# Attention tiles of a Mamba-attention-MoE kernel: the 64-row products of group 0 issued ahead of the 32-row products of groups 1 and 2

## The chip, the cores and the metric

The kernel runs on one core of a Trainium2 chip. A core has five engines that run side by side and meet at semaphores: TensorE (PE; its loads of weights are shown as PEld), VectorE (DVE), ScalarE (ACT), GpSimd (POOL) and SyncE (SP), which issues most DMAs. Each executes its own instructions in the order in which the program gives them. TensorE writes to PSUM, which has 8 banks of 128 partitions x 512 float32 values here; VectorE and ScalarE read it. The metric is the device time of one execution in microseconds (us), as the median of several runs. All data is float32.

## The reference

A state-space convolution layer (Mamba) is followed by an additive attention and a mixture of experts, over 8 batches of 4096 tokens with 128 channels. The change lies in the attention:

```
f = x @ W1[:h];  g = x @ W1[h:]
t = tanh(f[:, :, None, :] + g[:, None, :, :] + b1)      # 16 hidden units
scores = einsum('bija,a->bij', t, w2) + b2
e = exp(scores) * strictly_lower_triangle
w = e / (sum(e) + 1e-10)
out = w @ x
```

Every pair of a query token i and an earlier token j needs a sum over 16 values of tanh.

## The kernel before

The kernel does not compute the tanh. It writes the sum over the hidden units as a sum of three fractions N/D, one for each group of hidden units: group 0 has six units (64 sign patterns), groups 1 and 2 have five each (32 patterns). For each pair of tokens D is a product of exponentials, expanded to a sum over the sign patterns; so D and N are matrix products over 64 or 32 rows: `V` (one column per earlier token j) against `U` (one column per query i). The vectors are made in the first part (`mamba`, up to about 1,900 us of the span), kept in DRAM and brought back by `bring`.

`attend` (from about 1,907 to 6,062 us) works through 1,088 tiles of 128 earlier tokens x 512 queries, 136 per batch. 64 of them, on the diagonal, have only 256 columns; others near the diagonal are put together from two pieces. The order of the work is written out by hand; nothing reorders it. The loop at the end of `attend` runs over i, and an iteration works on several tiles:

- `rounds(cur, nxt)`, line 624 on TensorE: the D products of tile i+2 and the N products of tile i, six in all (each is a weight load and a product in two passes). In `V` and `U` the 64 rows of group 0 stand twice, at partitions 0 to 63 for D and 64 to 127 for N. The 32-row vectors stand at 0 to 31 (group 1, D), 32 to 63 (group 1, N), 64 to 95 (group 2, D) and 96 to 127 (group 2, N). Products in different rows of the array can run side by side: four with 32 rows, or two with 64.
- `inverses`, on ScalarE: line 643 takes the logarithm of the two D12 banks, line 644 that of the D0 bank, and line 646 (649 and 652 where the widths differ) takes exp(-x) of the three logarithms and of the scores of tile i-1 together.
- `causal`, line 666 on VectorE: the mask, on diagonal tiles.
- `ratios` and `scores`: line 657 (VectorE) multiplies the inverses of groups 1 and 2 by N12, line 658 (VectorE) that of group 0 by N0, line 659 (GpSimd) adds the fractions of groups 1 and 2, and line 671 (VectorE) adds that of group 0 to the sum.
- `weigh`, line 680 on TensorE: the weights of tile i-3 times the tokens, added up in the bank `av`.

Ahead of `rounds`, `advance("v", 3)` lets up to three steps of other work run, mostly on VectorE (finishing a block of queries, layer norm, the routing of the mixture of experts: lines 702 to 863); `advance("p", 1)` behind `weigh` issues at most one step on TensorE (lines 750, 720, 782, 845, 852).

PSUM is full: D12 and N12 (the products of groups 1 and 2) have two banks each, D0 and N0 (group 0) one each, `av` one and the other work one. Each has a single buffer. So a product into a bank waits until the reader of the iteration before is done: D12 for line 643, N12 for line 657, D0 for line 644, N0 for line 658. The readers in turn wait for the products: lines 643 and 657 for the group-2 product of their kind, the last into its banks.

After the attention come the experts and the output (from 6,062 us).

Of the kernel before, what the change touches and what calls it, by code (L numbers as in the profile page):

```python
# [44 lines left out]
def fast_path(  # L45
# [538 lines left out]
    def attend(aw, small, ap):  # L584
# [23 lines left out]
        def rounds(cur, nxt):  # L608


            parts = [(i, which) for i, which in ((nxt, 0), (cur, 1)) if i is not None]
            for i, which in parts:
                s = "DN"[which]
                (den, num)[which][i] = (
                    ap.tile([P, 2, CH], F32, tag=f"{s}12", name=f"{s}12_{i}"),
                    ap.tile([P, CH], F32, tag=f"{s}0", name=f"{s}0_{i}"),
                )
            for g, ab, rows, k in ((1, 1, 0, 32), (2, 1, 64, 32), (0, 0, 0, 64)):
                for i, which in parts:
                    b, ic, pieces = tiles[i]  # L620
                    r = slice(rows + k * which, rows + k * (which + 1))
                    t12, t0 = (den, num)[which][i]
                    for jb, q, n, at in pieces:
                        nc.tensor.matmul(  # L624
                            t12[:, g - 1, at : at + n] if g else t0[:, at : at + n],
                            lhsT=V[b, jb // NQ][r, ab, ts(jb % NQ, P)],
                            rhs=U[b, ic][r, ab, q : q + n],
                            start=True,
                            stop=True,
                        )  # L630
# [428 lines left out]
        for i in range(-2, n + 3):  # L1059
            cur = i if 0 <= i < n else None  # L1060
            nxt = i + 2 if i + 2 < n else None
            last = i - 1 if 0 <= i - 1 < n else None
            if 0 <= i < n:
                b, at = divmod(i, per)
                for more, g in begin.get(at, []):
                    if b + more < B:
                        bring(b + more, g)
            if i == -2:
                room(-2)
            if i < n:  # L1070
                room(i + 1)
            advance("v", 3)
            rounds(cur, nxt)
            if nxt is not None or last is not None:
                inverses(i, nxt, last)
            if i >= 2 and i - 2 < n:
                causal(i - 2)
            if cur is not None:
                ratios(cur)
                scores(cur)  # L1080
            if i >= 3:
                weigh(i - 3)
            advance("p", 1)
# [696 lines left out]
```

## Time and profile before

| what | value |
|---|---|
| median of 3 runs | 6327.22 us (6325.18 to 6329.36) |
| the profiled execution: its time | 6327.88 us |
| its span, first to last instruction | 6326.2 us, mean TensorE clock 0.946 |
| TensorE (PE) busy | 5825.4 us, 92% |
| VectorE (DVE) busy | 4935.0 us, 78% |
| ScalarE (ACT) busy | 4987.7 us, 79% |
| GpSimd (POOL) busy | 2023.4 us, 32% |

Windows of the profile, busy us of each engine in the stretch:

| window, us | PE | DVE | ACT | POOL | granted PE clock |
|---|---|---|---|---|---|
| 500 to 1000 (mamba) | 425.98 | 479.95 | 355.18 | 179.72 | 0.88 |
| 3000 to 3500 (attention) | 490.27 | 381.55 | 440.03 | 162.35 | 1.00 |
| 5000 to 5500 (attention) | 488.52 | 382.85 | 439.07 | 160.40 | 1.00 |

The lines of the profile read as follows. A group's line names line of the kernel, engine, operation, the tile written and those read with shapes, and how many; then busy us in all, mean ns of one, the idle us of the engine just ahead of them, and what ended that idle time. A line in order of time has start, duration, engine, line and operation; equal ones that follow each other are merged ("x2"), and in brackets stands the engine's idle time just before and its releaser. A float32 product shows as two instructions, one per pass. Busy time is counted from start to a modelled end for products, so TensorE can look fuller than it is.

### The profile page before, as it was taken

The page shows a single profiled execution, that of the slowest core. Times are in us where ns is not written, and L with a number is a line of the kernel's source. Part 1 is how long each engine was busy: PE and PEld are TensorE (multiplying, and loading weights), DVE is VectorE, ACT ScalarE, POOL GpSimd, SP SyncE. Part 2 cuts the span into 40 slices and gives each one's busy share as a digit, 9 for nine tenths or more (in the row PEclk, how much of TensorE's full clock was granted, in tenths as well). Part 3 has the DMA queues.
Part 4 walks back from the last instruction along what each step waited for, and adds up shares of the span by engine and source line. Part 5 has one row for each costly group of instructions (what it writes and reads, how often), then busy time and mean ns, then how long its engine had stood idle before and what let it go on. Part 6 is the DMA issues. An engine that isn't in the chain of part 4 may idle for free. (4 is left out here: it accounts for less than half of the span.)

```text
span 6326.2 us, 69220 instructions
## 1 busy us (share of the span) xinstructions
PE 5825.4 (92%) x22458; PEld 2224.5 (35%) x22458; DVE 4935.0 (78%) x7955; ACT 4987.7 (79%) x5657; POOL 2023.4 (32%) x1652
## 2 busy tenths in 40 slices
PE   7888888888869999999999999999999999999987
PEld 2333333333323333333333333333333333343335
DVE  7899999999956777777777777777777777777751
ACT  5667767767757998898899889889889988988941
POOL 2333333333312333333233233233333323323311
PEclk8888888888878999999999999999999999999989
DMA  2233333333341010101101101101100110110058
GB/s 81 74 110 117 125 122 126 122 127 127 115 145 60 24 44 26 32 12 49 29 24 32 37 21 44 34 24 31 38 21 24 40 38 24 32 34 24 15 190 303
DMA packets 182407, 426.64 MB, mean 67 GB/s; under 512 B 32579, under 2 KB 33235, under 8 KB 171283
## 3 DMA queue, kind: packets, MB, share of 16 engines
q1 hardware_dynamic: 172514, 403.48, 19.5%
q0 software_dynamic: 9376, 18.37, 0.8%
q8 instruction: 180, 2.95, 0.2%
q14 instruction: 193, 1.57, 0.1%
q10 hardware_dynamic: 144, 0.26, 0.0%
HBM read 295.12 MB, written 126.88 MB: 67 GB/s over the span
## 5 line engine op out<-in xcount | busy, mean ns | idle before, releaser
L624 PE MATMUL D<-U,V 32*128 32x512 f32 (+7 forms) x6912 | 2719.6, 606 | 15.6 <-DMA U<-uv_dram 13.3
L624 PE MATMUL N<-U,V 32*128 32x512 f32 (+7 forms) x6912 | 2354.7, 605 | 51.8 <-DVE mix L657 49.5
L659 POOL TENSOR_TENSOR mix<-mix 128x512 f32<-128x512 f32 (+1 forms) x1088 | 1350.0, 1241 | 2825.9 <-DVE mix L657 2702.7
L646 ACT ACTIVATE mix<-mix 128x2048 f32<-128x2048 f32 x973 | 1853.3, 1905 | 31.1
L671 DVE TENSOR_TENSOR mix<-mix,mix 128x512 f32<-128x512 f32 (+1 forms) x1088 | 736.5, 677 | 916.6 <-POOL mix L659 916.3
L643 ACT ACTIVATE mix<-D 128x1024 f32<-128x1024 f32 (+1 forms) x1088 | 1077.4, 990 | 440.2 <-PE N L624 391.7
L624 PEld LDWEIGHTS D<-U,V 32*128 32x128 f32 (+1 forms) x6912 | 879.4, 185 | 1420.0 <-issue 516.8
L657 DVE TENSOR_TENSOR mix<-mix,N 128x1024 f32<-128x1024 f32 (+1 forms) x1088 | 1284.2, 1180 | 29.5 <-PE N L624 22.8
L680 PE MATMUL av<-mix,tok 128*128 128x512 f32 (+3 forms) x2304 | 1208.9, 611 | 31.1 <-DVE sums L689 29.9
L624 PEld LDWEIGHTS N<-U,V 32*128 32x128 f32 (+1 forms) x6912 | 708.1, 184 | 274.0 <-DVE mix L657 237.5
L658 DVE TENSOR_TENSOR mix<-mix,N 128x512 f32<-128x512 f32 (+1 forms) x1088 | 722.0, 664 | 1.9 <-PE N L624 1.3
L644 ACT ACTIVATE mix<-D 128x512 f32<-128x512 f32 (+1 forms) x1088 | 632.3, 581 | 13.9 <-PE N L624 10.2
L680 PEld LDWEIGHTS av<-mix,tok 128*128 128x128 f32 x2304 | 350.8, 189 | 802.1 <-issue 691.1
L392 POOL TENSOR_TENSOR hc<-hs,rep 128x1024 f32<-128x1024 f32 x192 | 453.2, 2362 | 551.0 <-issue 377.4
L386 DVE TENSOR_TENSOR_SCAN hs<-da,hs,db 128x512 f32<-128x512 f32 x336 | 412.6, 1269 | 18.4 <-ACT da L373 10.0
L399 PE MATMUL py<-hc,ident 128*128 128x512 f32 x768 | 369.2, 633 | 0.9 <-ACT dt L337 0.9
L373 ACT ACTIVATE da<-dt,aneg 128x512 f32<-128x512 f32 x384 | 258.8, 687 | 122.8 <-DVE dt L352 79.9
L279 PE MATMUL px<-xt,wtap 128*128 128x512 f32 x512 | 346.7, 814 | 3.3 <-DMA xt<-in_x_dram 3.3
L326 PE MATMUL pdt<-bc,wdt 8*128 8x512 f32 x256 | 180.0, 824 | 138.7 <-DVE prod L320 85.8
L399 PEld LDWEIGHTS py<-hc,ident 128*128 128x128 f32 x768 | 166.7, 217 | 231.3 <-issue 219.8
L313 POOL DMA_DIRECT2D bc_dram<-bc x128 | 69.1, 544 | 512.8 <-ACT bc L311 512.8
L377 DVE TENSOR_TENSOR db<-dx,rep 128x1024 f32<-128x1024 f32 x192 | 228.0, 1215 | 0.1
(241 smaller groups left out, 5430.3 us busy)
## 6 DMA issues: line engine op xcount, KB each, us to landing
rep<-bc_dram SPq DMA_DIRECT2D x64, 1536.0 KB, 7.0
uv_dram<-uv SPq DMA_DIRECT2D x64, 768.0 KB, 3.5
xr<-in_x_dram SPq DMA_DIRECT2D x64, 256.0 KB, 3.3
k_dram<-tt SPq DMA_DIRECT2D x64, 256.0 KB, 7.2
k_dram<-tok SPq DMA_DIRECT2D x64, 256.0 KB, 7.3
U<-uv_dram SPq DMA_DIRECT2D x128, 128.0 KB, 2.9
V<-uv_dram SPq DMA_DIRECT2D x128, 128.0 KB, 2.9
U<-uv_dram SPq DMA_DIRECT2D x256, 64.0 KB, 2.0
```

The source lines that it names most:

```text
L386: nc.vector.tensor_tensor_scan(hs[:, h, :], ch[c].pop(("da", n, h)), db[:, h, :], first, ALU.mult, ALU.add)
L392: nc.gpsimd.tensor_tensor(hc, ch[c]["hs", n], ch[c]["rep"][:, 1, n, :].unsqueeze(1).to_broadcast([P, 2, CH]), ALU.mult)
L399: nc.tensor.matmul(py, lhsT=ident, rhs=ch[c]["hc", n][:, h, :], start=n == 0, stop=n == NR - 1)
L624: nc.tensor.matmul(t12[:, g - 1, at : at + n] if g else t0[:, at : at + n], lhsT=V[b, jb // NQ][r, ab, ts(jb % NQ, P)], rhs=U[b, ic][r, ab ...
L643: nc.scalar.activation(x[:, 1:3, lo:], d12[:, :, lo:], AF.Ln)
L644: nc.scalar.activation(x[:, 0, lo:], d0[:, lo:], AF.Ln)
L646: nc.scalar.activation(x[:, :, lo:], x[:, :, lo:], AF.Exp, scale=-1.0)
L657: nc.vector.tensor_tensor(r[:, 1:3, lo:], r[:, 1:3, lo:], n12[:, :, lo:], ALU.mult)
L658: nc.vector.tensor_tensor(r[:, 0, lo:], r[:, 0, lo:], n0[:, lo:], ALU.mult)
L659: nc.gpsimd.tensor_tensor(mix[k + 1][:, 3, lo:], r[:, 1, lo:], r[:, 2, lo:], ALU.add)
L671: nc.vector.tensor_tensor(s, s, mix[k - 2][:, 0, lo:], ALU.add)
L680: nc.tensor.matmul(av[0][:, q : q + n], lhsT=tok[b, jb // NQ][:, jb % NQ, :], rhs=mix[k + 1][:, 3, at : at + n], start=first, stop=last,)
```

## The change

One line in `rounds` changes: the order of the three groups. Group 0, the pair of 64-row products into D0 and N0, comes first; the 32-row products of groups 1 and 2 into D12 and N12 follow. The number and the sizes of the products, the banks and the readers stay; the order of the instructions on VectorE, ScalarE, GpSimd and SyncE is the same as before. On TensorE each iteration goes D0, N0, D1, N1, D2, N2, av where it went D1, N1, D2, N2, D0, N0, av.

```diff
-            for g, ab, rows, k in ((1, 1, 0, 32), (2, 1, 64, 32), (0, 0, 0, 64)):
+            for g, ab, rows, k in ((0, 0, 0, 64), (1, 1, 0, 32), (2, 1, 64, 32)):
                 for i, which in parts:
                     b, ic, pieces = tiles[i]
                     r = slice(rows + k * which, rows + k * (which + 1))
```

Some waits stand elsewhere for it. The first D0 product waits for line 644, the first N0 product for line 658. The 32-row products keep no wait for ScalarE or VectorE, since lines 643 and 657 come ahead of 644 and 658 on their engines; what is left to them is a wait for TensorE's own products of the tile before. Lines 644 and 658 wait for no product any more: lines 643 and 657 ahead of them wait for products that are issued behind D0 and N0.

## The prediction

> **What bounds the kernel now.** I read the page first, then the attention stretch (1,919 to 6,062 us, two thirds of the span) by groups of one shape, by waits, and in order of time. The chain that ended last is no help: it goes back only to 6,302 us. TensorE looks like the bound (98% busy in every attention window), but its busy time is modelled, and a product that has been issued early and stands alone counts as much as four that run side by side. So I ask each engine what it waits for. Groups by line and shape, with idle time and what ended it last in each row:
>
> ```profile
> L646 ACT ACTIVATE mix<-mix 128x2048 f32<-128x2048 f32 x966 | 1845.9, 1911 | 30.8
> L657 DVE TENSOR_TENSOR mix<-mix,N 128x1024 f32<-128x1024 f32 x1024 | 1240.8, 1212 | 29.5 <-PE N L624 22.8 <-ACT mix L649 5.8
> L643 ACT ACTIVATE mix<-D 128x1024 f32<-128x1024 f32 x1024 | 1039.9, 1016 | 427.8 <-PE N L624 379.3 <-PE D L624 25.0 <-DMA tt<-k_dram 12.8
> L671 DVE TENSOR_TENSOR mix<-mix,mix 128x512 f32<-128x512 f32 x1024 | 709.2, 693 | 878.6 <-POOL mix L659 878.4
> L658 DVE TENSOR_TENSOR mix<-mix,N 128x512 f32<-128x512 f32 x1024 | 695.6, 679 | 1.3 <-PE N L624 1.3
> ```
>
> ACT waits for TensorE (428 us ahead of line 643). VectorE almost never does: 29.5 us ahead of line 657 in 1,024 tiles, 1.3 us ahead of line 658. Its only regular idle time is the 0.86 us per tile in which line 671 waits for GpSimd's sum, and that lies inside its own chain 657, 659, 671. So VectorE's sequence sets the pace. One tile without other VectorE work, in order of time:
>
> ```profile
> 2370.95 1.21 DVE L657 TENSOR_TENSOR mix<-mix,N 128x1024 f32<-128x1024 f32 x1
> ...
> 2372.09 0.68 DVE L658 TENSOR_TENSOR mix<-mix,N 128x512 f32<-128x512 f32 x1
> ...
> 2372.13 0.69 PE L624 MATMUL D<-U,V 32*128 32x512 f32 x1
> ...
> 2372.22 0.69 PE L624 MATMUL N<-U,V 32*128 32x512 f32 x1
> ...
> 2373.29 0.69 PE L624 MATMUL D<-U,V 64*128 64x512 f32 x1
> ...
> 2373.62 0.69 DVE L671 TENSOR_TENSOR mix<-mix,mix 128x512 f32<-128x512 f32 x1 [0.85 <-POOL mix L659]
> 2374.23 1.21 DVE L657 TENSOR_TENSOR mix<-mix,N 128x1024 f32<-128x1024 f32 x1
> ...
> 2374.35 1.13 PE L680 MATMUL av<-mix,tok 128*128 128x512 f32 x2
> ```
>
> The reader is to see: the next tile's group-1 N product starts at 2372.22, right behind the end of line 657 (2370.95 + 1.21 = 2372.16) and well before line 658 ends (2372.77). The 64-row products follow 1.07 later, when line 658 is long done. So the N12 banks refill while VectorE works on, and line 657 finds its operand ready: from one line 657 to the next 3.28 us, all VectorE. From the starts of line 657 I count 1,087 intervals, 4,143.0 us, mean 3.81. Of the 1,024 behind a full tile, 420 are under 3.35 (mean 3.28), 128 from 3.35 to 3.80 (mean 3.60), 147 from 3.80 to 4.23 (mean 3.93) and 329 longer (mean 4.63: the routing work that VectorE has in these tiles). Of the 63 behind a tile of 256 columns, 47 are under 3.43, mean 3.07.
>
> How long TensorE needs from that N product to line 657 shows only where VectorE really waits:
>
> ```profile
> 2545.28 0.69 PE L624 MATMUL N<-U,V 32*128 32x512 f32 x1
> ...
> 2546.34 0.69 PE L624 MATMUL D<-U,V 64*128 64x512 f32 x1
> ...
> 2546.53 1.02 ACT L643 ACTIVATE mix<-D 128x1024 f32<-128x1024 f32 x1 [1.39 <-PE N L624]
> 2546.58 1.22 DVE L657 TENSOR_TENSOR mix<-mix,N 128x1024 f32<-128x1024 f32 x1 [0.98 <-PE N L624]
> ```
>
> From the 32-row start to line 657 it is 1.30 us, to line 643 1.25, and to the 64-row products 1.06 (two passes of 0.53).
>
> **The change, part by part.** Nothing is added or removed: six products per tile, and the order on VectorE, ScalarE, GpSimd and SyncE is the same; no DMA moves. Only TensorE's order changes, and with it what each wait holds up.
>
> *D0 first.* It waits for line 644 of the iteration before, which reads the only D0 buffer. The 32-row D products need no ACT wait any more, since line 643 ran before 644. Count from T, the start of the 32-row products: line 643 starts at T+1.25, 643 and 644 take 1.49 together (2374.22 to 2375.71 in the same tile, the second starting before the first ends), so D0 starts at T+2.8. TensorE has finished the four 32-row products at T+1.06 and av (1.06, row 2374.35 and the next D at 2375.40) at T+2.12. It then stands still for some 0.7 us. Queued behind D0 are all other products, av among them.
>
> *N0 second.* It waits for line 658 of the tile before, the last reader of the only N0 buffer, and the group-1 and group-2 products stand behind it on TensorE, which takes its products in order (D of 2372.13 went, N waited for line 657 and what follows waited with it). This closes a ring that was not there: line 657 to the end of 658, 2372.77 - 2370.95 = 1.82, I take 1.81 as the median; release of a bank to the N product 0.06 (2372.16 to 2372.22); N0 1.06; 32-row products to the next line 657 1.30. Sum 1.81 + 0.06 + 1.06 + 1.30 = 4.23 us. N0 starts at T+3.17, later than D0, so the N ring decides, not ACT (whose own three rows take 3.34 back to back).
>
> *What the ring covers.* Line 671 and the routing work run inside it, up to 4.23 - 3.28 = 0.95 us of routing per tile. An interval becomes the larger of 4.23 and what it is now. 420 x (4.23 - 3.277) = 400; 128 x (4.23 - 3.603) = 80; 147 x (4.23 - 3.930) = 44; the 329 longer ones nothing, as VectorE's own work covers the ring there; if that cover is partly wait, they would come down instead, by 132 us at most (329 x 0.40). Behind narrow tiles 657 and 658 take 1.01, so the ring is 3.43: 47 x 0.36 = 17. Together 542 us.
>
> *Other TensorE work* (pav, transposes, pl) fits in the idle 0.7 to 1.05 us before N0. Only the 28 groups of sixteen line-852 products (1.89 us) do not: N0 at T+4.0, interval 5.1 against 4.87 now, 28 x 0.25 = 7 us.
>
> *Gains.* Lines 644 and 658 find D0 and N0 early: idle of 13 and 1 us goes, but both now stand inside waiting rings, so I credit nothing.
>
> *The one unseen price* is a switch from 64-row to 32-row products. The seen switches (32 to 64 at 1.06 after a start, 64 to av 1.06, av to 32 1.06) are two bare passes, so zero to 0.01. Below nothing is excluded, since two passes cannot take less than 1.05. I take 0, and as upper end a ring of 4.40, which also covers a slightly lower clock: 683 us. Shortest latencies (ring 4.18): 505 us.
>
> [...]
>
> The profiled execution took 6327.9 us (span 6326.2), 0.7 above the median of 6327.2. 542 + 7 = 549 on the median gives 6876 us.
>
> **The clock.** The granted clock follows how busy TensorE is in a short stretch (columns: window, TensorE busy, clock, DMA share, GB/s):
>
> ```profile
> 1017.00:1020.40 3.40, 2.61 (x6) 1.00 0.62 230
> 1020.40:1023.80 3.40, 1.51 (x3) 0.83 0.21 51
> 1023.80:1027.20 3.40, 3.40 (x5) 0.50 0.96 275
> ```
>
> 77% busy keeps full clock, 44% is followed by half clock. In the new ring TensorE stands still some 0.7 of 4.23 us, 83% busy, so I expect 0.99 to 1.00 as now.
>
> **Rivals.**
> 1. *Clock falls.* The mamba stretch, 79 to 85% busy, has a mean of 0.87. Against: there the idle time comes in pieces of several us. At 0.87 the 2.2 us of products in the ring become 2.5, ring 4.56: +823 us, 7157 with the 7. Decides if windows under about half busy appear. 7%.
> 2. *D0 and N0 do not overlap.* If N0 starts only after D0 ends, T+3.9, the ring is 4.96: +1212 and the 7, 7546. Against: at 2372.13 and 2372.22 D and N ran side by side 0.09 out of step. 5%.
> 3. *Not slower: the new wait is already met when N0's turn comes, and the packed 32-row products serve line 657 earlier.* It then gains at most what line 657 waits for TensorE now, 22.8 us: 6304. Place: the start of N0. It decides if N0's turn comes 1.87 us or more behind the start of line 657. Now the next products start 1.18 after it (2374.23 to 2375.40), 0.7 too early. 4%, split between faster and same.
>
> **How the numbers follow.** The forecast (ring of 4.2 to 4.4) has 84%. Low end: ring 4.18 (-37) and half of the 132 us that the long intervals might give back (-66): 6773, I write 6775. High end: ring 4.40 gives 7017, and I go to 7040 toward rival 1. Rivals 2 and 3 and most of 1 stay out. A measurement of this kernel tells about 0.2% (13 us; the runs spread over 4). Faster 0.02, same 0.02, slower 0.96.
>
> **What would show it.** Right: idle ahead of line 657 rises from 29.5 to about 550 us and is ended by N of line 624; the 64-row N product starts 0.06 behind line 658, which now releases TensorE where 657 did; TensorE idles some 0.7 us ahead of D0, ended by line 644; idle ahead of 643 about doubles; intervals pile up at 4.23 where 3.28 stood; before 1,919 and behind the attention nothing moves. Wrong: intervals still at 3.28, a clock under 0.97 in the attention, or 32-row starts later than 1.08 behind N0.

## The result, and the profile after

The changed kernel takes 6905.6 us (median, 6899.8 to 6910.6) against 6328.3 for the kernel before (median of four runs): a ratio of 1.091, 95% interval 1.0897 to 1.0924. The profiled execution has a span of 6904.5 us, 578.3 more than before. The starts of line 657 tell where these lie: the 1,087 intervals between them add up to 4712.7 us where they were 4143.0, so 569.7 us came in the attention and 8.6 us ahead of it and behind it.

Groups by line and shape of the changed kernel, as shown of the kernel before:

```profile
L646 ACT ACTIVATE mix<-mix 128x2048 f32<-128x2048 f32 x966 | 1845.6, 1911 | 30.4
L657 DVE TENSOR_TENSOR mix<-mix,N 128x1024 f32<-128x1024 f32 x1024 | 1246.7, 1217 | 505.7 <-PE N L624 501.0
L624 PE MATMUL N<-U,V 32*128 32x512 f32 x3840 | 1102.3, 647 | 0.0
L624 PE MATMUL D<-U,V 64*128 64x512 f32 x1920 | 1082.7, 644 | 455.5 <-ACT mix L644 438.3 <-DMA U<-uv_dram 11.8
L624 PE MATMUL N<-U,V 64*128 64x512 f32 x1920 | 1081.6, 643 | 9.6 <-DVE mix L658 8.7
L643 ACT ACTIVATE mix<-D 128x1024 f32<-128x1024 f32 x1024 | 1047.6, 1023 | 952.6 <-PE N L624 895.8 <-PE D L624 43.8 <-PE fade_total L1020 12.8
L671 DVE TENSOR_TENSOR mix<-mix,mix 128x512 f32<-128x512 f32 x1024 | 709.2, 693 | 880.3 <-POOL mix L659 880.3
L658 DVE TENSOR_TENSOR mix<-mix,N 128x512 f32<-128x512 f32 x1024 | 695.8, 680 | 0.0
```

The three groups of products in the kernel before:

```profile
L624 PE MATMUL N<-U,V 32*128 32x512 f32 x3840 | 1091.6, 641 | 46.3 <-DVE mix L657 44.0
L624 PE MATMUL N<-U,V 64*128 64x512 f32 x1920 | 1088.3, 647 | 0.0
L624 PE MATMUL D<-U,V 64*128 64x512 f32 x1920 | 1087.6, 647 | 0.0
```

The readers did not become longer: 657, 643, 671 and 658 have the same mean to within 7 ns. The idle time ahead of line 657 went from 29.5 to 505.7 us, ended by N products. TensorE no longer waits for line 657 ahead of the 32-row N products; it now stands idle ahead of D0 (455.5 us, nearly all ended by line 644), and ScalarE's idle time ahead of line 643 more than doubled. N0's wait for line 658 hardly shows as idle time (9.6 us), because D0, issued just ahead of it, keeps TensorE busy meanwhile; its cost shows in the order of time.

One tile of the changed kernel in order of time:

```profile
2381.87 1.22 DVE L657 TENSOR_TENSOR mix<-mix,N 128x1024 f32<-128x1024 f32 x1 [0.48 <-PE N L624]
...
2382.81 0.59 ACT L644 ACTIVATE mix<-D 128x512 f32<-128x512 f32 x1
2383.01 0.68 DVE L658 TENSOR_TENSOR mix<-mix,N 128x512 f32<-128x512 f32 x1
...
2383.46 0.69 PE L624 MATMUL D<-U,V 64*128 64x512 f32 x1 [0.61 <-ACT mix L644]
...
2383.75 0.69 PE L624 MATMUL N<-U,V 64*128 64x512 f32 x1
2383.99 0.59 PE L624 MATMUL D<-U,V 64*128 64x512 f32 x1
2384.28 0.59 PE L624 MATMUL N<-U,V 64*128 64x512 f32 x1
2384.57 0.69 DVE L671 TENSOR_TENSOR mix<-mix,mix 128x512 f32<-128x512 f32 x1 [0.88 <-POOL mix L659]
2384.80 0.69 PE L624 MATMUL D<-U,V 32*128 32x512 f32 x1
...
2384.81 0.69 PE L624 MATMUL N<-U,V 32*128 32x512 f32 x1
```

Line 658 ends at 2383.69, and 0.06 later N0 starts. The 32-row products follow 1.05 later. VectorE's next line 657 is then this one, from the same view:

```profile
2386.03 1.22 DVE L657 TENSOR_TENSOR mix<-mix,N 128x1024 f32<-128x1024 f32 x1 [0.77 <-PE N L624]
```

VectorE was done with line 671 by 2385.26 and waited 0.77 us. From 657 to 657 it is 4.16 us; over the tiles the steps have medians of 1.82, 0.06, 1.06 and 1.30, sum 4.24.

Sorted by what the same interval was in the kernel before (mean us; the first four columns are the 1,024 intervals behind full tiles):

| kernel | 420, were under 3.35 | 128, 3.35 to 3.80 | 147, 3.80 to 4.23 | 329, longer | 63 behind narrow tiles |
|---|---|---|---|---|---|
| before | 3.277 | 3.603 | 3.930 | 4.632 | 3.240 |
| changed | 4.232 | 4.174 | 4.231 | 4.677 | 3.811 |

The granted clock stayed:

```profile
3000.00:3500.00 500.00, 447.02 (x1912) 171.40 (x1908) 350.14 (x598) 391.08 (x382) 142.45 (x115) 0.99 0.09 27
```

(Columns of this window: its length; busy us of PE, PEld, DVE, ACT and POOL; the clock; DMA share; GB/s.) TensorE is busy for 89% of it.

### The profile page after: what moved, and what is told of

Same layout as the page of the kernel before. It is cut to its first block, busy times and chain, and to the rows that moved or that the text cites. A ratio compares the mean times of both kernels' runs of the same rounds, so it can differ in the third digit from the quotient of the medians.

```text
span 6904.5 us, 69588 instructions
## 1 busy us (share of the span) xinstructions
PE 5956.4 (86%) x22458; PEld 2329.5 (34%) x22458; DVE 5003.3 (72%) x7955; ACT 5007.7 (73%) x5657; POOL 2022.1 (29%) x1652
## 5 line engine op out<-in xcount | busy, mean ns | idle before, releaser
L624 PE MATMUL D<-U,V 32*128 32x512 f32 (+7 forms) x6912 | 2421.9, 608 | 529.6 <-ACT mix L644 511.8
L624 PEld LDWEIGHTS D<-U,V 32*128 32x128 f32 (+1 forms) x6912 | 711.9, 185 | 1990.1 <-ACT mix L644 1193.5
```

The lines of the kernel that those rows point to most:

```text
L624: nc.tensor.matmul(t12[:, g - 1, at : at + n] if g else t0[:, at : at + n], lhsT=V[b, jb // NQ][r, ab, ts(jb % NQ, P)], rhs=U[b, ic][r, ab ...
```

## The experiments

Theory A is the prediction's: a ring through N0's only buffer (658, N0, the 32-row products, 657, 658). B puts the same wait into D0's buffer (644, D0, the 32-row products, 643, 644). C says that TensorE's own work sets the pace. Each run changes what its text names; the runs that give N0 a second buffer also move other work between the banks to make room for it.

### D0 released earlier

```diff
+                nc.scalar.activation(x[:, 0, lo:], d0[:, lo:], AF.Ln)
                 nc.scalar.activation(x[:, 1:3, lo:], d12[:, :, lo:], AF.Ln)
-                nc.scalar.activation(x[:, 0, lo:], d0[:, lo:], AF.Ln)
```

> The changed kernel, with line 644 (reads D0) put ahead of line 643 (reads D12) on ScalarE; everything is computed as before. Theory A (the ring of N0: the end of line 658, N0, the 32-row products, line 657, line 658) says that D0 is not what TensorE waits for last in a full tile: intervals between starts of line 657 that were under 3.35 us stay at 4.23, and only behind the narrow tiles, where 658 ends early and D0's wait for 644 is the later one (3.81 measured), they fall toward 3.43, some 18 us in all: 6885 to 6906 us. Theory B (the ring of D0: 644, D0, the 32-row products, 643, 644) says that D0 now comes free 1 us earlier and the ring falls to 3.0, below VectorE's own 3.28: 6330 to 6400 us.

Measured: 6875.3 us, ratio to the kernel before 1.0858 (1.084 to 1.0876). The 420 short intervals stay at 4.231; those behind narrow tiles fall from 3.811 to 3.510. Groups of this run:

```profile
L657 DVE TENSOR_TENSOR mix<-mix,N 128x1024 f32<-128x1024 f32 x1024 | 1246.2, 1217 | 505.2 <-PE N L624 500.6
L624 PE MATMUL N<-U,V 64*128 64x512 f32 x1920 | 1085.2, 645 | 89.4 <-DVE mix L658 86.0
L624 PE MATMUL D<-U,V 64*128 64x512 f32 x1920 | 1081.3, 643 | 11.9 <-DMA U<-uv_dram 11.9
```

The 438 us that TensorE waited for line 644 ahead of D0 are gone, and line 657 waits as before. So that wait cost nothing in full tiles: N0 was the later one. B falls. Behind narrow tiles it was the other way round, and there D0's ring did cost (19 us in the intervals; the median fell by 30, a little beyond the stated end).

### N0 released earlier

```diff
+            nc.vector.tensor_tensor(r[:, 0, lo:], r[:, 0, lo:], n0[:, lo:], ALU.mult)
             nc.vector.tensor_tensor(r[:, 1:3, lo:], r[:, 1:3, lo:], n12[:, :, lo:], ALU.mult)
-            nc.vector.tensor_tensor(r[:, 0, lo:], r[:, 0, lo:], n0[:, lo:], ALU.mult)
```

> The changed kernel, with line 658 (reads N0) put ahead of line 657 (reads N12) on VectorE; everything is computed as before. N0 comes free 1.1 us earlier, but GpSimd's sum (659), which waits for 657, starts 0.6 us later and VectorE's own sequence grows from 3.28 to 3.89 us. Theory A: the ring of N0 is broken, the intervals that stood at 4.23 fall to 3.9, while the long ones (VectorE's routing work) grow by 0.6; in all about 7015 us. Theory B, or a ring that does not run through line 658: nothing falls, the short ones stay at 4.23 and the long ones grow by 0.6, 7178 us.

Measured: 6954.2 us, ratio 1.0984 (1.0966 to 1.1003). The short intervals fell from 4.232 to 3.895, the long ones rose to 5.17. The numbers of the two lines are exchanged here: 658 reads N12.

```profile
L671 DVE TENSOR_TENSOR mix<-mix,mix 128x512 f32<-128x512 f32 x1024 | 708.7, 692 | 1510.2 <-POOL mix L659 1510.2
L658 DVE TENSOR_TENSOR mix<-mix,N 128x1024 f32<-128x1024 f32 x1024 | 1240.7, 1212 | 11.0 <-PE N L624 11.0
```

The wait for TensorE fell from 506 to 11 us, and the wait for GpSimd grew from 880 to 1510, which is what the swap costs: as A has it, a ring cut at N0 and another price paid. The sum was 61 us under the expectation, most of it since the long intervals stand only 0.54 above the kernel before, and those behind narrow tiles only 0.18, where 0.61 was reckoned.

### The products of line 680 left out, without and with a second N0 buffer

```diff
...
-            for jb, q, n, at in pieces:
-                nc.tensor.matmul(
-                    av[0][:, q : q + n],
...
             if last:
-                nc.vector.tensor_copy(sums[b, ic], av[0])
+                nc.vector.tensor_copy(sums[b, ic], tok[b, ic].rearrange("p q c -> p (q c)"))
```

> The changed kernel without the products of line 680: the weighted sum over earlier tokens is left out, and a copy of a token block stands in for it. TensorE loses 1.06 us per tile. Theory A: that time lay in the ring's idle place ahead of D0; the ring stays at 4.23, 6865 to 6906 us. Theory C (TensorE's own work is the bound, as its 98% busy in the kernel before suggest): up to 1.06 us per tile less, until VectorE's sequence holds it, that is down to 6330 us.

> As the run without line 680, whose bank is given to N0 as a second buffer; order of the products as in the changed kernel. Theory A: N0 no longer waits for line 658 of the tile before; the next wait is D0's for line 644, a ring of 0.06 + 1.06 + 1.25 + 1.49 = 3.86 us, and an interval is the larger of 3.86 and what VectorE needs: 6653 us. Theory B: D0's ring was the bound all along, so nothing changes against the run without line 680. Theory C: no change either.

Measured: 8148.9 us (ratio 1.2871, 1.2849 to 1.2892) and 7375.9 us (1.164, 1.1602 to 1.1679). All theories missed, for a reason that none of them had: TensorE with less to do lost its clock, which was 0.99 in the changed kernel, and is between 0.64 and 0.68 in the windows of the first run and between 0.72 and 0.74 in those of the second. Stretches of the first run, TensorE alone (length and busy us, clock, DMA share, GB/s):

```profile
3003.40:3006.80 3.40, 3.21 (x8) 0.50 0.00 0
3006.80:3010.20 3.40, 1.73 (x10) 0.50 0.00 0
...
3017.00:3020.40 3.40, 3.40 (x15) 0.58 0.00 0
3020.40:3023.80 3.40, 2.36 (x15) 1.00 0.00 0
```

At half clock a pass takes 1.01 us and the ring 6.05 (D0 at 3003.59 and at 3009.64). The times of these two runs therefore decide nothing between A, B and C. Their stretches at full clock tell more. In the first run 67 full-tile intervals that were under 4.23 in the kernel before lie wholly at full clock: they take 4.16 to 4.28, mean 4.22, though TensorE has 1.06 us less to do in each. So TensorE's own work is not what holds them there, and C falls for the changed kernel. In the second run 72 intervals of the 420 short ones lie wholly at full clock. None is over 3.93: 30 take 3.8 to 3.93, and 38 take 3.24 to 3.36, 35 of them right behind an interval of 3.7 or more. The 4.2 of the first run is gone with the second N0 buffer, as A says.

The second buffer was tried again with TensorE's load kept:

```diff
-            if first:
-                av[0] = ap.tile([P, CH], F32, tag="av", name=f"av{k}")
+            av[0] = bank(f"av{k}")
...
-                    start=first,
-                    stop=last,
+                    start=True,
+                    stop=True,
...
-                    ap.tile([P, CH], F32, tag=f"{s}0", name=f"{s}0_{i}"),
+                    ap.tile([P, CH], F32, tag=f"{s}0", bufs=1 + which, name=f"{s}0_{i}"),
...
```

> The changed kernel with two buffers for N0. The bank for it comes from av: the products of line 680 are all still issued, with the same sizes and operands, but each tile overwrites the last in the bank of the other work instead of adding up, so the weighted sum is left out and a copy of tokens stands in for most of it. TensorE's load per tile is that of the changed kernel, so the granted clock should stay near full (0.97 to 1.00 in the attention). Theory A (the ring of N0): it is cut, and the next wait is D0's for line 644, a ring of 3.86 us; an interval is the larger of 3.86 and VectorE's own need: intervals that were 3.28 in the kernel before and 4.23 in the changed one come to 3.85 to 3.95; 6630 to 6680 us. Theory B (the ring of D0 was the bound): 4.23 stays, about 6906 us.

Measured: 6695.4 us, ratio 1.0583 (1.0565 to 1.0601), clock 0.99 in the attention. The 420 short intervals stand at 3.823 with a median of 3.875, where A put D0's ring at 3.86; 4.23 is gone. 210 of the 577 us came back with one bank. Groups of this run (line 680 is 679 here):

```profile
L657 DVE TENSOR_TENSOR mix<-mix,N 128x1024 f32<-128x1024 f32 x1024 | 1245.4, 1216 | 302.3 <-PE N L624 300.2 <-issue 0.7
L624 PE MATMUL D<-U,V 64*128 64x512 f32 x1920 | 1088.6, 647 | 420.8 <-ACT mix L644 408.6 <-DMA U<-uv_dram 12.0
L624 PE MATMUL N<-U,V 64*128 64x512 f32 x1920 | 1085.0, 645 | 0.0
L679 PE MATMUL av<-mix,tok 128*128 128x512 f32 x1920 | 1080.8, 645 | 136.4 <-DVE tt L759 72.8 <-DVE xf L722 35.8 <-DVE sums L688 14.9
```

N0's buffer is the cause of the part above D0's ring: that is shown. That D0's buffer is the next wait fits the ring worked out (3.86 against 3.875) and TensorE's idle time ahead of D0, ended by line 644; no run frees both banks, so it is not shown by experiment. The time is 15 us above the expected range, and the long intervals are 4.79; the products of line 680, which share a bank with other work here, stand behind 136 us of new waits, which may be why.

### Room inside the ring: one more VectorE instruction

```diff
             r, (n12, n0) = mix[k - 2], num.pop(k)
+            nc.vector.tensor_tensor(spare, spare, spare, ALU.mult)
             nc.vector.tensor_tensor(r[:, 1:3, lo:], r[:, 1:3, lo:], n12[:, :, lo:], ALU.mult)
```

In the changed kernel and then in the kernel before:

> The changed kernel with one more VectorE instruction per tile, a 128x512 product of a spare tile with itself (0.61 us behind another instruction), issued right ahead of line 657; its result is not used. Theory A: the ring leaves VectorE 0.95 us idle in the tiles without routing work, so these stay at 4.23 and only the others grow: the larger of 4.23 and the interval of the kernel before plus 0.61, in all 7160 us. Without such a cover every tile grows by 0.61: 7570 us.

> The kernel before, with one more VectorE instruction per tile right ahead of line 657 (a 128x512 product of a spare tile with itself, 0.61 us), the counterpart of the same instruction in the changed kernel. Theory A: VectorE sets the pace without idle time, so every interval grows by 0.61 us: 6990 to 7030 us, that is 660 to 700 more, where the changed kernel paid 281. Theory C (TensorE sets the pace): the short tiles hide it, below 6700 us.

Measured: 7186.4 us in the changed kernel (281 more than without it) and 6933.1 us in the kernel before (604 more). The short intervals went from 4.232 to 4.246 and from 3.277 to 3.880. VectorE's wait for the products ahead of line 657 (661 in these runs) in the changed kernel, and then in the kernel before, each with the added instruction:

```profile
L661 DVE TENSOR_TENSOR mix<-mix,N 128x1024 f32<-128x1024 f32 x1024 | 1244.9, 1216 | 175.6 <-PE N L624 175.0
```

```profile
L661 DVE TENSOR_TENSOR mix<-mix,N 128x1024 f32<-128x1024 f32 x1024 | 1242.5, 1213 | 11.0 <-PE N L624 5.6 <-ACT mix L652 5.2
```

The same instruction is nearly free in a short tile of the changed kernel, where it takes the place of a wait (505.7 us without it), and costs its whole 0.60 us in the kernel before, where there was no wait to fill. In these tiles VectorE was the bound and is not any more; in the long ones it still is (4.68 to 5.22). The kernel before came out 57 us under the expected range, since narrow and long intervals grew by less (0.26 and 0.51).

### The other work moved into VectorE's wait for GpSimd

If VectorE sets the pace of the kernel before, its 0.86 us wait per tile is worth filling.

```diff
-            advance("v", 3)
+            if cur is None:
+                advance("v", 3)
             rounds(cur, nxt)
...
                 ratios(cur)
+                advance("v", 3)
                 scores(cur)
```

> The kernel before, with the up to three steps of other work of an iteration issued between lines 658 and 671, where VectorE waits 0.86 us for GpSimd, and no longer ahead of the products; everything is computed as before. If VectorE's sequence is what sets the pace of the kernel before, as the prediction says, the wait hides up to 0.86 us of routing work per tile. VectorE alone would then need 3.43 us per tile (5920 us in all); TensorE needs 3.19 and 0.43 of other products, 3.62 per tile, and ScalarE 3.34 to 3.55, so 6090 to 6170 us. If TensorE's products set the pace already (Theory C), nothing is gained: 6320 to 6340 us.

> The changed kernel with the same move of the other work. Theory A: tiles without much routing work stay at the ring of N0, 4.23, and gain nothing; the long ones (4.63 in the kernel before, 4.68 in the changed one) come down toward 4.23, as their routing work falls into the wait for GpSimd: about 6780 us. If VectorE's sequence and not the ring still set the pace in the changed kernel, the gain would be that of the kernel before, 160 to 240 us: 6670 to 6750 us.

Measured: 6361.4 us in the kernel before (ratio 1.006, 1.0043 to 1.0077) and 7404.2 us in the changed one (1.1703). Both expectations missed. Waits of the first run:

```profile
DVE mix L657 <- PE N L624: 329.3, 228, 2.9
...
PE pav L750 <- DVE tt L759: 90.0, 62, 2.0
PE pbf L720 <- DVE lnf L712: 85.8, 55, 2.0
```

The wait for GpSimd did shrink (899 to 487 us), but TensorE's step of an iteration now follows VectorE's steps of the same iteration and waits for them, with all products of the next tile behind it, and VectorE gets most of that back ahead of line 657 (22 to 329 us). The second run shows the same waits of TensorE, and VectorE's wait for N products ahead of line 657 grows from 502 to 1242 us; the time is 499 us longer than that of the changed kernel, where 125 us less were expected.

```profile
L657 DVE TENSOR_TENSOR mix<-mix,N 128x1024 f32<-128x1024 f32 (+1 forms) x1088 | 1293.7, 1189 | 1304.7 <-PE N L624 1242.5
```

If the waits of TensorE's step are the cause, both kernels gain when it is moved as well, to a place ahead of VectorE's:

```diff
-            advance("v", 3)
             rounds(cur, nxt)
...
                 ratios(cur)
-                scores(cur)
+            advance("p", 1)
+            advance("v", 3)
+            if cur is not None:
+                scores(cur)
             if i >= 3:
                 weigh(i - 3)
-            advance("p", 1)
```

> The kernel before, with the other work's TensorE step issued between N0 and the products of line 680, and its VectorE steps between lines 658 and 671; everything is computed as before. In the run that moved the VectorE steps alone, TensorE waited behind them (lines 750 and 720 for lines 759 and 712: 98 us in order of the profile's groups, with the products queued behind), because the TensorE step of an iteration then followed VectorE steps of the same iteration. Here it follows those of the iteration before, and VectorE reads its result when lines 657 and 658 are done. If that was the cause, the hidden 0.86 us shows: TensorE's 3.62 us per tile is the next bound, 6100 to 6200 us. If TensorE sets the pace in any case, 6320 to 6360 us.

In the next run `weigh` stands ahead of `advance("p", 1)`:

> As the run with both steps of the other work moved, but the TensorE step stands behind line 680 and not ahead of it; everything is computed as before. VectorE then reaches the step that reads it some 1.1 us before TensorE has made it, in tiles with such a step (some 460 of 1,088, not all with both): part of the gain goes into this new wait, 6150 to 6350 us.

Measured: 6016.2 us, ratio 0.9505 (0.9492 to 0.9518), and 6026.2 us, 0.9522 (0.9507 to 0.9537): both shorter than the kernel before and than the changed one. Waits of the first:

```profile
DVE mix L671 <- POOL mix L659: 493.8, 651, 0.9
...
DVE mix L657 <- PE N L624: 31.0, 48, 1.3
```

The wait for GpSimd is nearly halved (899 to 494 us) and none takes its place; the 329 long intervals fell from 4.63 to 3.60. Both ran under their expected ranges: the 3.62 us per tile that were set down for TensorE added up durations of small products that overlap (463 us in the attention of the kernel before, but they cover only 263), and the mean interval came to 3.52. The wait of VectorE for TensorE's step that the second was to pay is there (some 110 us ahead of its readers, against 24 in the first), but other waits are shorter, and the net cost is 10 us. What bounds the 3.52 was not tried: in the attention of the first (1,918 to 5,747 us) ScalarE is busy for 95% of the time and TensorE for 98%.

Last, the same two moves with the changed order:

> The changed kernel with the same two moves of the other work as the run of 6016 us (TensorE's step between the products of line 624 and line 680, VectorE's steps between lines 658 and 671); everything is computed as before. Theory A: the ring of N0 holds every full tile at 4.23 whatever VectorE has free, and only the long intervals come down to it: 6770 to 6810 us, so the order of the products costs some 760 us here and not 577. Without a ring the gain would be that of the kernel before, 313 us: about 6590 us.

Measured: 6791.6 us, ratio 1.0734 (1.0716 to 1.0752). Short intervals 4.239, long ones 4.268: nearly every full tile stands at the ring, and the 7404 us of the move without TensorE's step are gone, as the 6361 us were in the kernel before. The order of the products costs 775 us here, where VectorE needs less, and 577 where it needs more.

## Why the prediction was right

The forecast was 6876 us (6775 to 7040); 6905.6 was measured, so 577 us of slowdown against the 549 worked out.

- *VectorE sets the pace before, not TensorE's 98%.* Right: the added instruction cost 0.60 us in every short tile, and filling VectorE's wait gave 313 us. Theory C, that TensorE's own work sets the pace of the kernel before, falls with the first of these two: a bound TensorE would have hidden the instruction.
- *The N0 ring of 4.23 us.* Right to the hundredth: the 420 short intervals, 4.232. Their term was 400 us and measured 401.2 (420 x 0.955); 128 x 0.571 = 73 for 80, since 33 of these intervals lie ahead of a narrow tile and came only to 3.83; 147 x 0.301 = 44 for 44. The runs that move N0's release or give it a second bank show the mechanism, not only the number.
- *N0, not D0, decides.* Right in full tiles (N0 starts 0.29 behind D0, and an earlier D0 changes nothing).
- *Behind narrow tiles the ring is 3.43.* Wrong, 17 us set down and 36 measured (63 x 0.571). The step carried the shorter 657 and 658 into the N ring and forgot that D0's ring does not shrink with them: 3.81 was measured, and with D0 released early 3.51.
- *The 329 long intervals stay.* Nearly: 4.632 to 4.677, 15 us. Of these, 12 us lie in the intervals that touch a stretch at half clock, which the prediction did not count.
- *The 28 groups of sixteen line-852 products cost 7 us.* They cost about 6 beyond the ring, but that it came so near is luck. The prediction took all 28 intervals as 4.87 before and 5.1 after. They came to 4.93: 21 were 4.88 and grew by 0.05 each, and 7 were 3.61 (among the 128) and came to 4.92, which is 0.69 above the ring.
- *Nothing moves outside the attention.* Not quite: the first line 657 starts 3.9 us later and what follows the last takes 4.7 us more. These 9 us were not traced.
- *The unseen switch from 64-row to 32-row products costs nothing.* Right: 1.05 from N0 (2383.75) to the 32-row products (2384.80), two bare passes (N0's second starts at 2384.28, 0.53 behind the first). D0's last pass started at 2383.99, and at 0.53 a pass its rows would be free by 2384.52, an estimate; yet no 32-row product starts before N0 is through as well, and no time is added to that. The prediction's least of 1.05 for two passes was an estimate: from N0 to the first 32-row product 40 of the 960 products of 512 columns took 1.02 to 1.03 at full clock, against a median of 1.05.
- *The clock stays.* Right for this kernel (0.99; TensorE 89% busy and not 83%). The rival, that the clock falls, was to be decided by stretches under about half busy. Counted as in the last section (2,000 to 6,000 us), none in the changed kernel is under 63%; where they do appear, without line 680, the clock falls. The rival's fall of the clock is thus real: a third less work for TensorE (1.06 of 3.19 us of products per tile) was enough to bring it to 0.64 to 0.68.

The sum that was missed, 28 us, is thus mostly the narrow tiles (19) and what lies outside the attention (9); the long intervals (8 more) and the 128 (7 less) about cancel.

## What to carry to other kernels

With single buffers in PSUM, as here, the order of products should follow the order in which their banks are released: here a product that waits for the last reader, put first in a queue in which what stands behind it waits as well, closed a ring through every engine that takes part, and its length was the sum of the steps (medians of 4.24 us together, 4.23 measured), not the busy time of any one of them. To price such an edit, list for each interval what the pace-setter needs now and take the larger of that and the ring. Where the pace-setter has a short regular wait, put other work into it, but look at which queue then waits for that work: here the first attempt cost 0.6%, and the same move with the neighbour's step moved too gained 5%.

## What the runs showed of the hardware that was not expected

- *Less work for TensorE made the kernel slower.* Without line 680 TensorE has some 2.1 us of products in a ring of 4.23, and the kernel took 18% longer than with it (8148.9 against 6905.6 us). In these profiles the granted clock is either full or half, and it changes in steps of 3.41 us. Counted over these steps from the profile's clock and products (2,000 to 6,000 us of that run), full clock went to half 171 times, behind stretches with a median of 51% busy: 149 of the 150 stretches at full clock that were under 52% busy were followed by half clock. It came back 171 times, each behind a stretch of 89% or more; but some 180 stretches at half clock were as busy and did not bring it back, so that alone does not decide. In between the clock mostly kept what it had: of the stretches 60 to 85% busy, 137 of 150 at full clock were followed by full clock, and all 199 at half clock by half. So in that run the same busy share went with full clock behind full and with half clock behind half. The changed kernel, median 86% busy, lost the clock 12 times in 4,000 us, and the kernel before 14 times.
- *Passes of different rows did not keep to the program's order.* A float32 product shows as two passes, 0.53 us apart (D1 at 2372.13 and 2372.66 in the kernel before). At 2372.22 to 2372.24 (kernel before) the first passes of N1, D2 and N2 start together, and the second pass of N1, a product that stands ahead of D2 in the program, only at 2372.76. A wait, on the other hand, held back the other rows as well: D2 and N2 stood behind N1's wait for line 657, 0.1 behind D1 (2372.13), where in the changed kernel, with no such wait, all four start within 0.02 (2384.80 to 2384.82).
